# A message-passing layer on a graph: gathered rows transposed 128 edges at a time, and rounds of sums moved behind the next group's products

## The chip, the cores and the metric

The kernel runs on one core of one Trainium2 chip. The time is that of one launch on the device, in microseconds (us), and smaller is better; three runs of the kernel before took 1334.07, 1339.48 and 1347.27 us, with a median of 1339.48 us.

The engines have short names here: PE is TensorE doing matmuls, PEld its loads of weights, DVE is VectorE, ACT ScalarE, POOL GpSimd, SP SyncE. L596 is line 596 of the kernel before. "Issue" as the cause of a wait means that the profile shows nothing that the engine waited for.

## The reference: what is computed

There are 6250 nodes with 128 features (`x`), and 100000 edges with a source and a destination; the edges come sorted by destination. For every edge a small network of three layers turns the two nodes' features into a message; messages are averaged by destination; a second network updates each node; the sum of input and update is normalized. All in float32.

```
msg_in = concat(x[src], x[dst])                      # 100000 x 256
h  = relu(msg_in @ Wm1 + bm1)                        # 100000 x 256
h  = relu(h @ Wm2 + bm2)                             # 100000 x 256
agg = segment_sum(h @ Wm3 + bm3, dst) / max(count, 1)
upd = relu(concat(x, agg) @ Wn1 + bn1) @ Wn2 + bn2
out = layernorm(x + x + upd)
```

## The kernel before, in words

**Preparation.** `msg_in @ Wm1` is the sum of a product that depends on the source alone and one that depends on the destination alone. So the kernel makes two tables in DRAM: `atab` (node times the upper half of Wm1) and `btab` (node times the lower half, split into three bf16 terms). It also transposes the lists of sources so that 128 edges lie on 128 partitions: `src_f` is the list as numbers, copied from the integers at L381 to L383, then transposed by `source_columns` (L455) into `srcT`. The copy at L382 also reorders: within 512 edges, tile `u` gets the 64 edges `u` of the first 256 on partitions 0 to 63, and the 64 edges `u` of the second 256 on partitions 64 to 127.

**The loop over groups.** The edges are cut into 196 groups of 512 (4 tiles of 128; GT = 4). For each group `k` these steps exist:

- `gather` (L530): four indirect DMAs, issued by POOL, bring the group's 4 x 128 rows of `atab` to `rows`, of which there are 4 buffers; they are issued two groups ahead in the program.
- `open_layer` (L558): PE transposes the gathered rows into two PSUM banks. Each bank takes 256 edges. For each half of the hidden units (`c`), for each tile `u`, for each half `h` of the partitions, one transpose of 64 edges x 128 units goes to 64 columns of bank `h`: 2 x 4 x 2 = 16 transposes (L569), each with a load of 128 columns of weights (the data are the weights, the identity is what moves).
- `first_layer` (L574): on top of it four bf16 products (L582) add the destinations' terms; a one-hot matrix `oht` picks the row of `btab` that an edge needs. These contract over 64 partitions. Then ACT takes both banks through four relus to `h1` (L588).
- `second_layer` (L591), for the group before, `k - 1`: 8 float32 matmuls, two to a tile, which the profile shows as 16 records (L596). DVE takes each of the two banks (two tiles) to one of six buffers `h2` with a maximum (L598).
- `some_sums` (L792): a round of sums. PE multiplies a one-hot matrix of 32 nodes with a tile of `h2`, and four windows of 32 nodes lie side by side in one PSUM bank, `sum_bank` (L604, 8 records to a round). After a batch's last round ACT copies the bank to `part` (L609).
- `turn_sums` (L802): three transposes of `part` (L617) on PE; DVE adds the windows to `acc`, the sums of all nodes (L624).
- every fourth group two more tiles of `btab` (L904), up to about the middle of the kernel, and from there on pieces of the node update (`node_stage`, L687; matmuls at L700, L715, L719, L727) in `node_step`.

**What sets the order.** PE's instructions stand in the order of the program, so do those of ACT and DVE in the loop (`manual_schedule`, L411 and L413). For a step `k` below 196 it is: first layer of `k`, the gather of `k + 2`, second layer of `k - 1`, `node_step`, `turn_sums(k)`, `some_sums(k)` (L873 to L889). Which round of which batch falls in which step is set by `deal` (L758): a batch of four groups (groups 0 to 71) has its first round in the step where its last group's second layer stands, one round in the step after, and two in the next; batches of two groups (72 to 147) and of one (148 to 183) come later behind the second layer. There are 196 rounds and 97 turns in all. PE, ACT and DVE meet through semaphores alone.

Of the kernel before, what the change touches and what calls it, by code (L numbers as in the profile page):

```python
# [20 lines left out]
P = 128  # L21
# [15 lines left out]
def kernel(  # L37
# [36 lines left out]
    nc = tc.nc  # L74
# [4 lines left out]
    GT = 4  # L79
    GE = GT * P  # L80
    HE = 2 * P
    NG = -(-E // GE)
# [6 lines left out]
    NQ = 2 * WN  # L89
# [46 lines left out]
    ident = const.tile([P, P], F32, name="ident")  # L136
# [98 lines left out]
    def scratch(at, n, p=P):  # L235
        return acc_flat[:p, at:at + n]
# [52 lines left out]
    halves = [slice(h * NQ, (h + 1) * NQ) for h in range(2)]  # L289
# [9 lines left out]
    with tc.tile_pool(name="prep", bufs=1) as prep, tc.tile_pool(name="pp", bufs=3, space=PSUM) as pp, tc.tile_pool(  # L299
        name="pb", bufs=5, space=PSUM  # L300
    ) as pb:
        src_i, dst_i = (scratch(AT + k * 2 * GE, 2 * GE, R).bitcast(I32) for k in range(2))
        real, src_f, rel = (scratch(AT + k * 2 * GE, 2 * GE, R) for k in (2, 3, 4))
# [45 lines left out]
        def index_work():  # L349
# [29 lines left out]
                              rel.bitcast(BF16)[:, :2 * GE].rearrange("r (s h e) -> r s h e", s=2, h=2))  # L379
            yield  # L380
            for s in range(2):  # L381
                nc.vector.tensor_copy(src_f[:, s * GE:(s + 1) * GE].rearrange("r (u h e) -> r u h e", u=GT, h=2),  # L382
                                      src_i[:, s * GE:(s + 1) * GE].rearrange("r (h u e) -> r u h e", h=2, u=GT))  # L383
            yield
            over = more[:, 1]
            nc.vector.tensor_add(over, most, quad)
# [128 lines left out]
    with edge, tc.tile_pool(name="wk", bufs=2) as wk, tc.tile_pool(  # L515
# [8 lines left out]
        def bank():  # L524
            return banks.tile([P, 2, H], F32, name="bank")

        def flat_bank():
            return bank().rearrange("p t h -> p (t h)")
# [16 lines left out]
        def hot_rows(rb):  # L545
            oht = wk.tile([P, 2, HE], BF16, name="oht")
            nc.vector.tensor_scalar(oht, rb, iota_p, None, op0=ALU.is_equal)
            return oht
# [9 lines left out]
        def open_layer(ag, nt, xt=None):  # L558
            nh = nt // 2
            ph = [bank() for _ in range(nh)]  # L560
            for c in range(HC):
                if xt is not None:
                    for h in range(nh):
                        nc.tensor.matmul(ph[h][:, c, :], w1[:, 0, c * P:(c + 1) * P], xt[:, h * HE:(h + 1) * HE],
                                         start=(c == 0), stop=False, skip_group_check=True)
                    continue
                for u in range(GT):
                    for h in range(nh):
                        nc.tensor.matmul(ph[h][:, c, u * NQ:(u + 1) * NQ], ag[halves[h], u, c * P:(c + 1) * P],  # L569
                                         ident[halves[h], halves[h]], is_transpose=True,  # L570
                                         start=(c == 0 and u == 0), stop=False, skip_group_check=True)
            return ph

        def first_layer(ag, bw, oht, nt, nk, ph=None):  # L574
# [65 lines left out]
        def make_hot(p):  # L640
            ohts[p] = hot_rows(rels[p // 2][:, 2 * (p % 2):2 * (p % 2) + 2])
            make_nodes(p)

        def make_nodes(p):
            ohs[p] = hot_nodes(dloc[:, 2 * p:2 * p + 2, :].rearrange("p g j -> p (g j)"), 2, iota_n)
# [146 lines left out]
        def some_sums(k):  # L792

            for gs, t, n in rounds.pop(k, ()):
                windows = [w for g in gs for w in units_of(g)]
                if t == 0:
                    sum_banks[gs[0]] = flat_bank() if k > NG else p3.tile([P, 2 * H], F32, name="sum_bank")
                sum_tile(sum_banks[gs[0]], windows, t, n)
                if t == n - 1:
                    parts[gs[0]] = part_of(sum_banks.pop(gs[0]), len(windows)), len(windows)  # L800

        def turn_sums(k):  # L802
            for g in turns_at.pop(k, ()):
                part, nw = parts.pop(g)
                pt = turned(part, nw)
                add_up(pt, load_bases(uniti[0:1, unit_at[g]:unit_at[g] + nw], nw, ENG.DVE))
# [50 lines left out]
        for g in range(-4, NG + 14, 2):  # L857
            for i in range(g + 4, min(g + 6, NG)):
                terms[i] = fetch(load_bases(tilei[0:1, i * GT:(i + 1) * GT], NTS[i], ENG.SP), nk_of(i))
            if g < -2:  # L860
                continue
            if (g + 2) % 4 == 0 and g + 6 < NG:
                rels[(g + 6) // 4] = places((g + 6) // 4)
            if g < 0:
                continue
            if g == 0:
                first_step()
            for k in (g, g + 1):
                if k < NG:
                    s = st[k] = {}  # L870
                    if k == 1:
                        xts[1] = open_layer(None, NTS[1], xts[1])
                    s["h1"] = first_layer(rows.pop(k, None), terms.pop(k), ohts[k // 2][:, k % 2], NTS[k], nk_of(k),  # L873
                                          xts.pop(k, None))
                    if k == 0:
                        next_rows()
                    if k == 2:
                        nc.scalar.copy(*pace(5))
                if 2 * XS <= k + 2 < NG:
                    rows[k + 2] = gather(sources(k + 2))  # L880
                if k % 2 == 0 and k + 2 < NG:
                    make_hot(k // 2 + 1)
                if 0 <= k - 1 < NG:
                    second_layer(st.pop(k - 1)["h1"], h2s[(k - 1) % len(h2s)], NTS[k - 1])
                if k < NG:
                    node_step(k)
                if k <= NG:
                    turn_sums(k)
                some_sums(k)  # L889
                if k > NG:  # L890
                    turn_sums(k)
                if k % 2 == 0 and 2 <= k and k + 5 < NG:
                    nc.vector.tensor_copy(*pace(k + 5))
                if k >= NG:
                    node_step(k)
            if g < 6:
                clear(8)
            if g == 0:
                more_rows()
            t0 = B_EARLY + (g - B_FROM) // 2  # L900
            if g >= B_FROM and (g - B_FROM) % 4 == 0 and t0 < NT:
                pbt = bank()
                for a in range(min(2, NT - t0)):
                    nc.tensor.matmul(pbt[:, a, :], xT[:, (t0 + a) * P:(t0 + a + 1) * P], w1[:, 1, :],  # L904
                                     start=True, stop=True)
                b_terms(t0, pbt, b_rows, b_rest)
            if g == 18:
                late_weights()
            if g == 60:
                made_weights()  # L910
            if g == NG + 2:
                with tc.high_priority():
                    again = nc.values_load(
                        again_i[0:1, 0:1], min_val=0, max_val=1,
                        skip_runtime_bounds_check_because="0 or 1, by its computation")
# [8 lines left out]
        with tc.If(again > 0, preferred_fallthrough_block=True, label="again"):  # L924
            with tc.For_i(0, NG, 1) as g:
# [13 lines left out]
                with tc.For_i(0, more, 1):  # L939
# [8 lines left out]
                    ag, bw = gather(idx), fetch(load_bases(ti, GT, ENG.SP), 2)  # L948
# [44 lines left out]
```

## Time and profile before

| | us |
|---|---|
| median of three runs | 1339.48 |
| lowest and highest run | 1334.07, 1347.27 |
| the profiled execution's own time | 1338.36 |
| its span, from the first to the last instruction | 1336.6 |
| PE busy | 1236.1 (10031 matmul records) |
| PE loading weights | 925.5 |
| POOL busy | 748.7 |
| DVE busy | 618.2 |
| ACT busy | 441.9 |
| granted TensorE clock, mean | 0.981 |

How to read the views: a row of the groups gives line, engine, operation, the tiles written and read, shape and count, then busy time in us and the mean of one in ns, then the idle time of the engine ahead of it and what ended most of that. A row of the timeline gives a start and a length in us, with what was merged and how often; lengths on PE reach to the modelled end of the last matmul, so neighbours overlap. A row of the windows gives the busy us of each engine in a stretch and in brackets the number of instructions. Matmuls are pipelined: a mean of 392 ns is the time from entering to leaving, not what one adds to the stream.

### The profile page before, as it was taken

To read this page: it belongs to the slowest core of one execution; us is meant where nothing else is said; L and a number is where in the kernel's file an instruction comes from. 1 tells how busy PE (TensorE), PEld (TensorE's weight loads), DVE (VectorE), ACT (ScalarE), POOL (GpSimd) and SP (SyncE) were. 2 spreads that over 40 slices of the span, in tenths; PEclk is the share of its full clock that TensorE was granted. 3 is DMA by queue.
4 is the path that set the end of the run, shared out by engine and by line. 5 is a ranking of instruction groups with operands and counts; after the bars stand their busy time and mean duration, and the time that the engine had idled before them with its cause. 6 is when DMAs were issued, how large, how long until landed. Compare 5 with 4: busy or idle time off the path is not lost.

```text
span 1336.6 us, 27771 instructions
## 1 busy us (share of the span) xinstructions
PE 1236.1 (92%) x10031; PEld 925.5 (69%) x10032; DVE 618.2 (46%) x1551; ACT 441.9 (33%) x1102; POOL 748.7 (56%) x795
## 2 busy tenths in 40 slices
PE   9779998998999999999899999999999999999997
PEld 7556666666666666676677777777777777777675
DVE  6443333433334333434466554444445556556553
ACT  4432323323323323333333423333233333333331
POOL 2366665665665666656555465565655555555550
PEclk9879999999999999999999999999999999999998
DMA  8544434444434434434444344444444434443330
GB/s 287 177 125 134 132 108 127 130 115 129 133 106 128 135 107 125 134 106 131 126 118 119 114 125 128 118 120 129 118 118 118 115 109 118 109 123 110 106 91 4
DMA packets 107617, 163.90 MB, mean 123 GB/s; under 512 B 26367, under 2 KB 71549, under 8 KB 107457
## 3 DMA queue, kind: packets, MB, share of 16 engines
q0 software_dynamic: 37504, 102.29, 27.7%
q1 hardware_dynamic: 69425, 59.50, 14.0%
q8 instruction: 82, 1.34, 0.4%
q14 instruction: 62, 0.51, 0.1%
q10 hardware_dynamic: 544, 0.26, 0.1%
HBM read 142.48 MB, written 19.86 MB: 121 GB/s over the span
## 4 chain that ended last, share of the span: by engine, by line
PE 89%; issue 7%; DVE 2%; another core or an unknown queue 1%; DMA 1%; ACT 0%; SPq 0%; DVEq 0%
PE bank L596 54%; PE bank L569 9%; PE sum_bank L604 9%; PE bank L582 4%; PE bank L617 2%; PE pbt L431 2%; PE bank L727 2%; PE bank L700 2%; PE bank L719 2%; PE bank L715 2%; PE bank L904 1%; PE pt L448 0%; DVE acc L660 0%; DVE x_sb L598 0%
## 5 line engine op out<-in xcount | busy, mean ns | idle before, releaser
L596 PE MATMUL bank<-w,h 128*128 128x256 f32 x3128 | 768.7, 392 | 67.2 <-issue 64.6
L596 PEld LDWEIGHTS bank<-w,h 128*128 128x128 f32 x3128 | 581.7, 192 | 212.3 <-issue 131.1
L533 POOL DMA_INDIRECT rows<-atab,srcT x392 | 374.9, 956 | 260.6 <-issue 90.4
L533 POOL DMA_INDIRECT rows<-atab,srcP x384 | 364.2, 949 | 277.9 <-issue 126.5
L588 ACT ACTIVATE h<-bank,b 128x256 f32<-128x256 f32 x782 | 306.5, 476 | 395.6 <-remote 189.3
L598 DVE TENSOR_TENSOR x_sb<-bank,nb 128x512 f32<-128x512 f32 x263 | 181.0, 691 | 401.7 <-PE bank L596 233.7
L598 DVE TENSOR_TENSOR h_more<-bank,nb 128x512 f32<-128x512 f32 x128 | 88.3, 692 | 177.5 <-PE bank L596 75.0
L569 PEld LDWEIGHTS bank<-ident,rows 64*128 64x128 f32 x3096 | 112.7, 140 | 77.7 <-issue 56.8
L569 PE MATMUL bank<-ident,rows 64*128 64x64 f32 x3096 | 139.3, 230 | 0.0
L624 DVE TENSOR_TENSOR acc<-acc,bank 128x96 f32 x382 | 96.7, 253 | 51.7 <-PE bank L569 16.5
L604 PE MATMUL sum_bank<-x_sb,oh 128*32 128x257 f32 x1044 | 104.1, 393 | 3.0 <-issue 1.6
L609 ACT COPY part<-sum_bank 128x257 f32<-128x257 f32 x96 | 35.8, 373 | 197.0 <-PE bank L582 75.4
L582 PE MATMUL bank<-oht,terms 64*128 64x128 bf16 (+1 forms) x1132 | 82.6, 237 | 14.5 <-issue 10.9
L604 PE MATMUL sum_bank<-h_more,oh 128*32 128x257 f32 x512 | 59.1, 391 | 1.2 <-DVE h_more L598 0.6
L604 PEld LDWEIGHTS sum_bank<-x_sb,oh 128*32 128x32 f32 x1044 | 28.1, 108 | 41.7 <-issue 34.1
L582 PEld LDWEIGHTS <-terms 64*128 64x128 bf16 x1132 | 44.1, 97 | 16.1 <-issue 13.8
L617 PE MATMUL bank<-ident,part 128*128 128x128 f32 (+1 forms) x291 | 47.3, 271 | 0.5 <-ACT part L609 0.5
L745 ACT ACTIVATE y<-y,sh,rs 128x128 f32<-128x128 f32 (+3 forms) x50 | 22.1, 487 | 67.0 <-DVE sh L743 26.6
L695 DVE RECIPROCAL x_sb<-x_sb 128x256 f32<-128x256 f32 (+3 forms) x26 | 43.0, 1655 | 0.9
L617 PEld LDWEIGHTS bank<-ident,part 128*128 128x128 f32 (+1 forms) x291 | 36.6, 139 | 9.3 <-ACT part L609 1.0
L552 DVE TENSOR_TENSOR oh<-iota_n,dloc 128x256 f32<-128x256 f32 x98 | 40.8, 417 | 3.6 <-ACT dloc L838 3.6
L737 ACT ACTIVATE sd<-mv,eps 128x2 f32<-128x2 f32 (+3 forms) x26 | 7.7, 295 | 97.6 <-DVE mv L735 49.5
(157 smaller groups left out, 625.0 us busy)
## 6 DMA issues: line engine op xcount, KB each, us to landing
terms<-btab SPq DMA_DIRECT2D x566, 32.0 KB
places<-reltab SPq DMA_DIRECT2D x98, 128.0 KB
btab<-x_sb SPq DMA_DIRECT2D x10, 768.0 KB
rows<-atab,srcT POOLq DMA_INDIRECT x392
atab<-acc SPq DMA_DIRECT2D x12, 512.0 KB
rows<-atab,srcP POOLq DMA_INDIRECT x384
xr<-in_x_dram SPq DMA_DIRECT2D x23, 128.0 KB
out_dram<-y SPq DMA_DIRECT2D x23, 128.0 KB
```

Source lines behind the costliest of these rows:

```text
L533: nc.gpsimd.indirect_dma_start(out=ag[:, j, :], out_offset=None, in_=atab[:, :], in_offset=bass.IndirectOffsetOnAxis(ap=idx[:, j:j + 1], a ...
L552: nc.vector.tensor_tensor(oh[:, :ng].rearrange("p g j n -> p (g j) n"), iota.to_broadcast([P, ng * GT, WN]), dl.rearrange("p (j o) -> p j ...
L569: nc.tensor.matmul(ph[h][:, c, u * NQ:(u + 1) * NQ], ag[halves[h], u, c * P:(c + 1) * P], ident[halves[h], halves[h]], is_transpose=True, ...
L582: nc.tensor.matmul(ph[h][:, c, k * n:(k + 1) * n], bw[halves[h], k, c * P:(c + 1) * P], oht[halves[h], k * n:(k + 1) * n], start=False, st ...
L588: nc.scalar.activation(h1[:, c, h * HE:(h + 1) * HE], ph[h][:, c, :], AF.Relu, bias=b1[:, c:c + 1])
L596: nc.tensor.matmul(ph2[:, j - j0, :], h1[:, c, j * P:(j + 1) * P], w2[:, c, :], start=(c == 0), stop=(c == HC - 1))
L598: nc.vector.tensor_tensor(h2[:, j0:j0 + 2, :H], ph2, nb2.to_broadcast([P, 2, H]), op=ALU.max)
L604: nc.tensor.matmul(pg[w * WN:(w + 1) * WN, :H + 1], oh, h2, start=(t == 0), stop=(t == total - 1), skip_group_check=True)
L609: nc.scalar.copy(part[:nw * WN], pg[:nw * WN, :H + 1])
L617: nc.tensor.matmul(pt[:, c, :q], rows, ident[:q, :q], is_transpose=True, start=True, stop=True, skip_group_check=True)
L624: nc.vector.tensor_add(window, window, pt[:, :, j * WN:(j + 1) * WN])
L695: nc.vector.reciprocal(rc, rc)
```

## The change

Three edits. The transposes of gathered rows become 8 of 128 edges x 128 units, each over all 128 partitions, and tile `j` goes to columns of bank `j // 2`. For this the copy of the sources leaves the edges in their order. And in a step `k` below 196 the rounds that stood at the end of step `k - 1` now stand behind the first layer of `k`, ahead of the second layer of `k - 1`; from step 196 on the rounds of the step itself come behind the second layer as well, and the turns come last in every step.

```diff
@@ index_work
             for s in range(2):
-                nc.vector.tensor_copy(src_f[:, s * GE:(s + 1) * GE].rearrange("r (u h e) -> r u h e", u=GT, h=2),
-                                      src_i[:, s * GE:(s + 1) * GE].rearrange("r (h u e) -> r u h e", h=2, u=GT))
+                nc.vector.tensor_copy(src_f[:, s * GE:(s + 1) * GE], src_i[:, s * GE:(s + 1) * GE])
@@ open_layer
-                for u in range(GT):
-                    for h in range(nh):
-                        nc.tensor.matmul(ph[h][:, c, u * NQ:(u + 1) * NQ], ag[halves[h], u, c * P:(c + 1) * P],
-                                         ident[halves[h], halves[h]], is_transpose=True,
-                                         start=(c == 0 and u == 0), stop=False, skip_group_check=True)
+                for j in range(nt):
+                    nc.tensor.matmul(ph[j // 2][:, c, j % 2 * P:(j % 2 + 1) * P], ag[:, j, c * P:(c + 1) * P],
+                                     ident, is_transpose=True, start=(c == 0 and j % 2 == 0), stop=False,
+                                     skip_group_check=True)
@@ the loop over groups
+                some_sums(k - 1)
                 if 0 <= k - 1 < NG:
                     second_layer(st.pop(k - 1)["h1"], h2s[(k - 1) % len(h2s)], NTS[k - 1])
                 if k < NG:
                     node_step(k)
-                if k <= NG:
-                    turn_sums(k)
-                some_sums(k)
-                if k > NG:
-                    turn_sums(k)
+                if k >= NG:
+                    some_sums(k)
+                turn_sums(k)
```

On PE, around the first round of a batch of four groups, the order before is this (L596 is the second layer, L604 the round, L569 the transposes, L582 the destinations' products; `h_2766` is the `h1` of the group before):

```order
L596 MATMUL bank<-w_151,h_2766 128x256 x8
L604 MATMUL sum_bank<-h_more,oh 32x257 x2
L604 MATMUL sum_bank<-x_sb,oh 32x257 x2
L569 MATMUL bank<-ident,rows 128x64 x16
L582 LDWEIGHTS terms
L582 MATMUL bank<-oht,terms 128x256
...
L596 MATMUL bank<-w_151,h_2859 128x256 x8
```

The same place with the change (with two lines fewer ahead, so L594 is the second layer, L602 the round, L567 the transposes, L580 the products):

```order
L594 MATMUL bank<-w_151,h_2516 128x256 x8
L567 MATMUL bank<-ident,rows 128x128 x8
L580 LDWEIGHTS terms
L580 MATMUL bank<-oht,terms 128x256
...
L602 MATMUL sum_bank<-h_more,oh 32x257 x2
L602 MATMUL sum_bank<-x_sb,oh 32x257 x2
L594 MATMUL bank<-w_151,h_2611 128x256 x8
```

The round has moved past the transposes and the products of the next group, 16 transposes have become 8 of twice the width, and the products now stand between transposes and round instead of between transposes and second layer.

On ACT, where a batch ends, the order before is this (L588 are the relus of the first layer, L609 the copy of the finished sums, L256 a copy for `btab`):

```order
L588 ACTIVATE h_2988<-bank,b_153 128x256 x4
L609 COPY part<-sum_bank 128x257
L588 ACTIVATE h_3047<-bank,b_153 128x256 x4
L256 CAST x_sb<-bank 128x2x256
L259 CAST x_sb<-x_sb 128x2x256
```

With the change (L586 are the relus, L607 the copy):

```order
L586 ACTIVATE h_2720<-bank,b_153 128x256 x4
L586 ACTIVATE h_2765<-bank,b_153 128x256 x4
L607 COPY part<-sum_bank 128x257
L256 CAST x_sb<-bank 128x2x256
L259 CAST x_sb<-x_sb 128x2x256
```

The copy has moved behind the next group's four relus. DVE's and POOL's instructions stand in the same order as before; on SP a few loads ahead of the loop's middle and the stores of the output move by some places.

## The prediction

> **What bounds the kernel now.** First the page's head and its chain of waits:
>
> ```profile
> span 1336.6 us, 27771 instructions
> PE 1236.1 (92%) x10031; PEld 925.5 (69%) x10032; DVE 618.2 (46%) x1551; ACT 441.9 (33%) x1102; POOL 748.7 (56%) x795
> PE 89%; issue 7%; DVE 2%; another core or an unknown queue 1%; DMA 1%; ACT 0%; SPq 0%; DVEq 0%
> ```
>
> PE is busy for 92% of the span and carries 89% of the chain that ends last; no other engine comes near. So what the change adds to PE counts, unless PE has idle time that it can go into. The costliest groups, then the timeline of PE through one step that runs without a stall, show what PE does with a group:
>
> ```profile
> L596 PE MATMUL bank<-w,h 128*128 128x256 f32 x3128 | 768.7, 392 | 67.2 <-issue 64.6
> L569 PE MATMUL bank<-ident,rows 64*128 64x64 f32 x3096 | 139.3, 230 | 0.0
> 604.18 3.92 PE L596 MATMUL bank<-w,h 128*128 128x256 f32 x16
> 608.02 0.64 PE L604 MATMUL sum_bank<-x_sb,oh 128*32 128x257 f32 x8
> 608.60 0.71 PE L569 MATMUL bank<-ident,rows 64*128 64x64 f32 x16
> 609.15 0.38 PE L582 MATMUL bank<-oht,terms 64*128 64x256 bf16 x4
> 609.46 3.72 PE L596 MATMUL bank<-w,h 128*128 128x256 f32 x16
> 613.01 0.49 PE L617 MATMUL bank<-ident,part 128*128 128x128 f32 x3
> ```
>
> The starts are what counts: from 604.18 to 609.46 a whole group passes in 5.28 us, and its 16 transposes take 608.60 to 609.15, 0.55 us. 3096 of them at 16 to a group are 193.5 groups (two groups open otherwise, one is half as long).
>
> But the groups pass more slowly than that. Windows of the whole loop, PE and PEld busy and the number of records first, then the same for L596 alone, 16 records to a group:
>
> ```profile
> 250.00:350.00 100.00, 91.78 (x734) 65.31 (x734) 37.03 (x80) 31.23 (x76) 60.56 (x65) 1.00 0.43 125
> 650.00:750.00 100.00, 97.62 (x825) 78.15 (x825) 60.24 (x151) 35.56 (x92) 52.99 (x56) 1.00 0.42 119
> 750.00:850.00 100.00, 95.07 (x844) 73.85 (x843) 50.76 (x131) 34.83 (x92) 58.21 (x62) 1.00 0.42 120
> 150.00:650.00 500.00, 462.88 (x3658) 328.51 (x3658) 189.58 (x424) 157.05 (x385) 304.85 (x322) 0.99 0.42 124
> 650.00:1250.00 600.00, 568.94 (x4944) 444.98 (x4943) 319.66 (x825) 202.61 (x531) 340.36 (x358) 1.00 0.42 118
> 250.00:350.00 100.00, 63.02 (x258) 46.94 (x258) 1.00 0.43 125
> 650.00:750.00 100.00, 52.74 (x224) 41.30 (x224) 1.00 0.42 119
> 750.00:850.00 100.00, 59.11 (x248) 45.68 (x249) 1.00 0.42 120
> 150.00:650.00 500.00, 319.65 (x1277) 236.67 (x1275) 0.99 0.42 124
> 650.00:1250.00 600.00, 342.92 (x1438) 265.84 (x1439) 1.00 0.42 118
> ```
>
> From 150 to 650 us 1277 / 16 = 79.8 groups pass, 6.27 us each, with PE idle for 37.1 us, 0.46 to a group. From 650 to 1250, where the node update has joined, 89.9 groups take 6.67 us each with 31.1 us idle, 0.35 to a group. The idle time is of one sort: stops of up to a microsecond inside L596 that end in "issue" (64.6 of the 67.2 us in its row above), as here:
>
> ```profile
> 615.73 1.33 PE L596 MATMUL bank<-w,h 128*128 128x256 f32 x5 [0.16 <-issue]
> 618.09 0.38 PE L596 MATMUL bank<-w,h 128*128 128x256 f32 x1 [1.02 <-issue]
> 619.58 1.67 PE L596 MATMUL bank<-w,h 128*128 128x256 f32 x7 [1.12 <-issue]
> ```
>
> What makes them no view says. One thing can be read off: they shrink where a group has more work. With 16.1, 15.5 and 14.0 groups in the windows at 250, 750 and 650 us, PE's busy time to a group is 5.69, 6.13 and 6.97 us, and its idle time 0.51, 0.32 and 0.17. From the first to the second 0.19 of 0.44 us is taken up by idle time (43%), from the second to the third 0.15 of 0.84 (18%). I take a third.
>
> **The change part by part.** *The transposes.* 16 of 64 edges become 8 of 128. The trace has the new form, 128 x 128 in float32, eight in a row, and a passage from full-height float32 matmuls to L582:
>
> ```profile
> 38.54 0.81 PE L431 MATMUL pbt<-w,xT 128*128 128x256 f32 x3
> 39.19 1.04 PE L465 MATMUL px<-ident,acc 128*128 128x128 f32 x8
> 46.88 1.99 PE L564 MATMUL bank<-acc,w 128*128 128x256 f32 x8
> 48.81 0.39 PE L582 MATMUL bank<-oht,terms 64*128 64x256 bf16 x4
> L465 PE MATMUL px<-ident,acc x8: 272/272/273, 39.2 to 40.0; 128*128 128x128 f32 x8
> ```
>
> The last of the eight takes 0.27 us to leave, so they enter (1.04 - 0.27) / 7 = 0.11 us apart, and eight cost 0.88 us where sixteen cost 0.55. The sixteen are cheap because the two halves of the partitions run side by side.
>
> *The seams.* Where PE goes over to another part of the array the trace shows a bubble. A matmul of 256 columns enters 0.22 us after the one ahead ((3.72 - 0.38) / 15 at L596) and leaves 0.38 after it entered, so it lets the next in 0.16 before it leaves. The round's last leaves at 608.02 + 0.64 = 608.66 and so lets go at 608.50; the old transposes start at 608.60, a bubble of 0.10. The new ones follow second layer, turn or L904, which use the whole array as they do: L431's last leaves at 39.35, lets go at 39.19, and there L465 starts, with no bubble. In return L582 gets one, which now follows the old transposes at once: L564's last leaves at 48.87, lets go at 48.71, and L582 starts at 48.81, 0.10 later. The round's other seams, to L596 and to L582, change partners but not in number. So to a group: before 0.10 + 0.55 = 0.65, now 0.88 + 0.10 = 0.98, **+0.33 us; over 193.5 groups +63.9 us**. The new form's price is measured on this chip in a stream; its bounds are the rounding of the rows, 0.31 to 0.35 (60 to 68 us).
>
> *The moved rounds.* The first round of a batch of four needs the maximum that DVE has just been handed (L598); before, it stood right behind the second layer that feeds DVE. PE's waits at L604 for it, and the rows of ACT for the other end of the batch:
>
> ```profile
> DVE x_sb L598: 4.9, 5
> DVE h_more L598: 2.2, 4
> L588 ACT ACTIVATE h<-bank,b 128x256 f32<-128x256 f32 x782 | 306.5, 476 | 395.6 <-remote 189.3
> L609 ACT COPY part<-sum_bank 128x257 f32<-128x257 f32 x96 | 35.8, 373 | 197.0 <-PE bank L582 75.4
> ```
>
> These 7.1 us can go at most, since DVE now has transposes and products, over 1 us, to finish in; the least is nothing, if another stop takes their place. I take 4 off. The price of the move: `part` is now copied behind four relus of the next group, 4 x 306.5 / 782 = 1.57 us, and then 0.37. The turn that waits for it comes behind the second layer, 609.46 to 613.01 = 3.55 us of PE, so 1.6 us of cover are left; if they were gone, a tenth of a microsecond would cost 97 turns 10 us. Behind a waiting turn stand the next group's transposes, and POOL waits for their buffers. I take nothing. No DMA, no load of a register and no instruction of DVE or POOL moves past another; SP's few moved stores are waited for by nobody in the loop.
>
> *The copy of the sources* is two casts before the loop, each within one microsecond of DVE beside PE's table products; a plain one may be shorter or not, within 1 us, and lies off the path. Nothing.
>
> *Sum:* 63.9 - 4 = +60 us of work on PE, of which a third, 20, goes into idle time: +40. Against the profiled execution: 1336.6 + 40 = 1376.6 of span, 1.8 around it (1338.36 - 1336.6), and 1.1 from there to the median of the runs shown (1339.48): **1380 us, 3% slower**. With 18 to 43% taken up and the transposes' bounds the forecast's own range is 1372 to 1395.
>
> **The rivals.** *Nothing is taken up.* The stops could come with the clock on the wall, whatever PE has to do; then all 60 to 64 us show: 1400 to 1403. For it: they are found in windows of every kind. Against it: their share falls as the work rises.
>
> *All of it is taken up.* Something that is not PE could pace the loop at 6.27 us (POOL and its gathers, say, with 304.85 us busy for 79.8 groups, 3.8 each, and a pause behind every one). Then +0.33 fits into 0.46 and 0.35 idle: 1340, within 1%. Against it: the second stretch has another pace, and in its fullest window only 0.17 is idle.
>
> *Faster: PE is short of instructions, not of time.* In the first stretch PE gets 7316 records in 500 us, 68 ns to each. A group loses 16 records (8 loads, 8 matmuls) of 92. If the stops come from feeding PE, fewer records fill its queue sooner, and the moved round no longer holds the queue up behind a wait. Then the 68.2 us idle in these 1100 us go, 78 over the loop's 1259 us (from 52.8 to 1312.1 us): 1336.6 + 60 - 78 + 2.9 = 1321. It decides only if more than nine tenths of the stops go. Against it: in the second stretch records come at 61 ns, and the 16 transposes pass at 34 ns each with their loads. The Trainium skill, page "TensorE: Matmul & The Clock Gate", section "Wait — 56ns, not 53.3ns?", says that a sequencer decoding in software spends about 62 ns per matmul, which binds when the array's work is shorter. By that figure, as an estimate, 46 matmuls of a group would need 2.8 us, well under 6.27, so that the loop as a whole would not be bound by it; the transposes' own 34 ns disagree with it too.
>
> *Loads that no longer overlap.* Eight full-height loads could each wait for the transpose ahead: 139 ns as in the row below, on top of 0.11, makes 2.0 us instead of 0.88, and +215 us more, 1595.
>
> ```profile
> L617 PEld LDWEIGHTS bank<-ident,part 128*128 128x128 f32 (+1 forms) x291 | 36.6, 139 | 9.3 <-ACT part L609 1.0
> ```
>
> The Trainium skill, the same page, section "The mechanism" in Part 3, has a rule that says so: loads overlap running matmuls only where the row groups differ. The row of L465 speaks against it: with a load to each, they enter 0.11 us apart.
>
> **How the numbers follow.** The forecast 0.46; nothing taken up 0.24; all of it 0.14; faster 0.13; loads in series 0.03. Within 1% is about what a measurement of this kernel can tell from no change, since the three runs spread over 1%. Faster by over 1% 0.13, the same 0.14, slower 0.46 + 0.24 + 0.03 = 0.73. The range for 8 in 10 goes from the faster case's price, 1320, leaving out half of it, to 1410, above the case without take-up: 1320 to 1410.
>
> **What would show it.** Right: the new transposes number 1548, eight in a row about 1.04 us long in the timeline; the products (L582) begin 0.98 us after the first of them; a step without stall takes 5.6 us; PE's busy time up by some 60 us, its idle time down by some 20, most of it in L596's "issue"; the waits of L604 for DVE near zero; L617 without waits for `part`. Wrong: a pitch of the transposes far from 0.11; idle time in "issue" that is unchanged (1403) or gone (1321); groups at 6.27 us as before in the first stretch (1340); new waits of PE for ACT at L617.

## The result, and the profile after

The changed kernel takes 1454.28 us (four runs, 1451.15 to 1461.07) against 1339.28 us for the kernel before: ratio 1.0866, interval 1.0829 to 1.0902. It is slower, as forecast, but by 115 us instead of 40, and beyond the range (1320 to 1410). The ratios in this document are of the runs that the record counts as fast, the medians of all runs. The head of its page, the chain of waits and two of its groups:

```profile
span 1454.3 us, 24724 instructions
PE 1317.2 (91%) x8483; PEld 1017.8 (70%) x8484; DVE 608.1 (42%) x1551; ACT 437.2 (30%) x1102; POOL 750.4 (52%) x795
PE 82%; issue 6%; another core or an unknown queue 5%; ACT 3%; DVE 3%; DMA 1%; SPq 0%; DVEq 0%; ACTq 0%
L594 PE MATMUL bank<-w,h 128*128 128x256 f32 x3128 | 750.1, 393 | 8.5 <-issue 8.4
L567 PE MATMUL bank<-ident,rows 128*128 128x128 f32 x1548 | 215.0, 281 | 13.2 <-issue 12.9
```

PE's busy time is up by 81 us (1236.1 to 1317.2), and the rest of the span, in which PE is idle, has grown too, from 100 to 137 us, where the forecast had it shrink by 20. The stops inside the second layer are all but gone (64.6 us in "issue" before, 8.4 now), but others have come. What PE waited for, in us, with the number of times and the longest:

```profile
PE bank L615 <- ACT part L607: 42.5, 15, 4.4
PE bank L580 <- issue: 18.3, 23, 1.3
PE sum_bank L602 <- issue: 16.7, 20, 2.4
PE bank L567 <- issue: 12.9, 24, 1.7
PE bank L615 <- issue: 10.2, 7, 3.4
```

The turn (L615) waits 42.5 us for `part`, where it waited 0.5 us before. Where no stop falls into a step, the change is what the prediction worked out. The timeline of PE, in the same kernel:

```profile
610.88 3.72 PE L594 MATMUL bank<-w,h 128*128 128x256 f32 x16
614.44 1.04 PE L567 MATMUL bank<-ident,rows 128*128 128x128 f32 x8
615.41 0.39 PE L580 MATMUL bank<-oht,terms 64*128 64x256 bf16 x4
615.73 0.64 PE L602 MATMUL sum_bank<-x_sb,oh 128*32 128x257 f32 x8
616.30 3.72 PE L594 MATMUL bank<-w,h 128*128 128x256 f32 x16
```

The eight transposes come right behind the second layer, last 1.04 us, and the products start 0.97 after the first of them. Now the pace over the loop, all engines first (PE and PEld busy ahead), then L594 alone with 16 records to a group:

```profile
150.00:650.00 500.00, 462.04 (x2902) 351.02 (x2901) 176.04 (x401) 149.04 (x369) 291.17 (x305) 0.97 0.40 117
650.00:1250.00 600.00, 553.46 (x3756) 434.23 (x3755) 274.93 (x710) 177.66 (x473) 307.72 (x323) 0.97 0.38 107
150.00:650.00 500.00, 288.30 (x1225) 0.97 0.40 117
650.00:1250.00 600.00, 313.31 (x1300) 0.97 0.38 107
```

A group takes 500 / (1225 / 16) = 6.53 us in the first stretch (6.27 before) and 600 / (1300 / 16) = 7.38 in the second (6.67 before). Most of the loss lies where the node update has joined, the stretch with the least idle time before.

### The profile page after: what moved, and what is told of

Same layout as the page of the kernel before. It is cut to its first block, busy times and chain, and to the rows that moved or that the text cites. A ratio compares the mean times of both kernels' runs of the same rounds, so it can differ in the third digit from the quotient of the medians.

```text
span 1454.3 us, 24724 instructions
## 1 busy us (share of the span) xinstructions
PE 1317.2 (91%) x8483; PEld 1017.8 (70%) x8484; DVE 608.1 (42%) x1551; ACT 437.2 (30%) x1102; POOL 750.4 (52%) x795
## 4 chain that ended last, share of the span: by engine, by line
PE 82%; issue 6%; another core or an unknown queue 5%; ACT 3%; DVE 3%; DMA 1%; SPq 0%; DVEq 0%; ACTq 0%
PE bank L594 44%; PE bank L567 12%; PE sum_bank L602 8%; PE bank L580 5%; PE bank L615 3%; ACT h L586 3%; PE pbt L430 2%; PE bank L725 2%; PE bank L717 2%; PE bank L698 1%; PE bank L901 1%; PE bank L713 1%; DVE x_sb L596 1%; DVE acc L622 1%
## 5 line engine op out<-in xcount | busy, mean ns | idle before, releaser
L594 PE MATMUL bank<-w,h 128*128 128x256 f32 x3128 | 750.1, 393 | 8.5 <-issue 8.4
L594 PEld LDWEIGHTS bank<-w,h 128*128 128x128 f32 x3128 | 591.0, 194 | 171.2 <-issue 83.5
L586 ACT ACTIVATE h<-bank,b 128x256 f32<-128x256 f32 x782 | 307.2, 475 | 539.5 <-remote 169.3
L596 DVE TENSOR_TENSOR x_sb<-bank,nb 128x512 f32<-128x512 f32 x263 | 177.8, 690 | 509.8 <-PE bank L594 152.2
L567 PE MATMUL bank<-ident,rows 128*128 128x128 f32 x1548 | 215.0, 281 | 13.2 <-issue 12.9
L567 PEld LDWEIGHTS bank<-ident,rows 128*128 128x128 f32 x1548 | 187.5, 146 | 30.8 <-issue 18.5
L596 DVE TENSOR_TENSOR h_more<-bank,nb 128x512 f32<-128x512 f32 x128 | 86.2, 689 | 242.7 <-remote 107.3
L602 PE MATMUL sum_bank<-x_sb,oh 128*32 128x257 f32 x1044 | 112.0, 409 | 18.0 <-issue 13.8
L580 PE MATMUL bank<-oht,terms 64*128 64x128 bf16 (+1 forms) x1132 | 85.5, 247 | 20.5 <-issue 18.3
L615 PE MATMUL bank<-ident,part 128*128 128x128 f32 (+1 forms) x291 | 51.9, 290 | 55.9 <-ACT part L607 42.5
L615 PEld LDWEIGHTS bank<-ident,part 128*128 128x128 f32 (+1 forms) x291 | 35.5, 145 | 74.4 <-ACT part L607 49.5
L580 PEld LDWEIGHTS <-terms 64*128 64x128 bf16 x1132 | 35.3, 96 | 58.3 <-issue 54.6
L602 PEld LDWEIGHTS sum_bank<-x_sb,oh 128*32 128x32 f32 x1044 | 29.2, 110 | 48.8 <-issue 33.1
L602 PE MATMUL sum_bank<-h_more,oh 128*32 128x257 f32 x512 | 59.9, 392 | 3.3 <-issue 2.8
L607 ACT COPY part<-sum_bank 128x257 f32<-128x257 f32 x96 | 37.4, 389 | 75.5 <-remote 45.8
L720 ACT ACTIVATE x_sb<-bank,bu 128x256 f32<-128x256 f32 (+3 forms) x52 | 21.0, 456 | 79.5 <-remote 44.9
```

Of the source, the lines that this page charges most:

```text
L567: nc.tensor.matmul(ph[j // 2][:, c, j % 2 * P:(j % 2 + 1) * P], ag[:, j, c * P:(c + 1) * P], ident, is_transpose=True, start=(c == 0 and j ...
L580: nc.tensor.matmul(ph[h][:, c, k * n:(k + 1) * n], bw[halves[h], k, c * P:(c + 1) * P], oht[halves[h], k * n:(k + 1) * n], start=False, st ...
L586: nc.scalar.activation(h1[:, c, h * HE:(h + 1) * HE], ph[h][:, c, :], AF.Relu, bias=b1[:, c:c + 1])
L594: nc.tensor.matmul(ph2[:, j - j0, :], h1[:, c, j * P:(j + 1) * P], w2[:, c, :], start=(c == 0), stop=(c == HC - 1))
L596: nc.vector.tensor_tensor(h2[:, j0:j0 + 2, :H], ph2, nb2.to_broadcast([P, 2, H]), op=ALU.max)
L602: nc.tensor.matmul(pg[w * WN:(w + 1) * WN, :H + 1], oh, h2, start=(t == 0), stop=(t == total - 1), skip_group_check=True)
```

## The experiments

The kernel before does not take the same time everywhere, and that became the main finding. On some chips, here **sort A**, it takes 1337 to 1339 us: the prediction's profile and the result are of this sort, and the runs on chips 10 and 3. On others, **sort B**, it takes 1190 us: chips 2, 6, 11 and 12. PE is busy there for 99% of the span (in the moved rounds alone, which take as long). No numbered chip was used in more than one set of runs, so the record can't tell a lasting difference between chips from a state that a chip is in for some minutes; "sort" stands for either. Each kernel is compared with the kernel before that ran beside it:

| | sort A (before 1338) | sort B (before 1190) |
|---|---|---|
| wide transposes alone | 1350.17, +13 | 1278.56, +89 |
| moved rounds alone | 1406.29, +69 | 1189.81, 0 |
| both: the change | 1455.05, +118 | 1253.35, +63 |
| the change, turns a step later | 1454.95, +118 | 1263.56, +74 |
| before, no gathers | 1202.62, -136 | - |
| moved rounds, no gathers | - | 1189.40, -1 |
| the change, no gathers | - | 1253.50, +64 |

**The parts alone, on sort B.** The first edit is the transposes and the copy of the sources without the move; the second is the move without the transposes:

```diff
+                some_sums(k - 1)
                 if 0 <= k - 1 < NG:
                     second_layer(st.pop(k - 1)["h1"], h2s[(k - 1) % len(h2s)], NTS[k - 1])
...
-                if k <= NG:
-                    turn_sums(k)
-                some_sums(k)
-                if k > NG:
-                    turn_sums(k)
+                if k >= NG:
+                    some_sums(k)
+                turn_sums(k)
```

> The kernel before with the wide transposes alone; rounds and turns stand as before. Theory A (the turn that now follows its round after one second layer only is what costs beyond the transposes' own time, since PE's signals of finished work reach ACT up to 7 us late): the price of the transposes, 0.31 us a group, shows, so 1385 to 1400 us; PE waits less than 3 us for part at the turn; idle time in issue stays near 80 us. Theory B (the wide transposes themselves make the stops worse, whatever the order): 1430 or more, with the stops spread over all lines.

> The kernel before with the moved rounds alone; sixteen half transposes to a group. Theory A: PE waits some 40 us for part at the turn, and then runs at a lower clock for a while, so 1385 to 1405 us. Theory B: the moved rounds are harmless or save a few us, 1330 to 1345, and the waits for part stay below 10 us.

Measured: 1278.56 us (ratio 1.0744, 1.0726 to 1.0762) and 1189.81 us (1.0003, 0.9993 to 1.0012), beside 1189.65. The forecasts were made for sort A and can't be judged by these runs. On this chip the moved rounds cost nothing, and the transposes cost more without them than with them. PE's timeline of the wide transposes alone shows why:

```profile
610.16 0.64 PE L602 MATMUL sum_bank<-h_more,oh 128*32 128x257 f32 x8
610.73 1.09 PE L567 MATMUL bank<-ident,rows 128*128 128x128 f32 x8
611.75 0.40 PE L580 MATMUL bank<-oht,terms 64*128 64x128 bf16 x8
```

Here the transposes stand behind a round: it lets its follower in at 610.16 + 0.64 - 0.16 = 610.64, so they start 0.09 late, and the products follow after 1.02 instead of 0.97. The round has its own seam to the second layer ahead of it as before. Together that is an estimated 0.14 us at each of the 166 places where a round stands ahead, 23 us, of the 25 between 1278.56 and 1253.35 (the changed kernel on sort B, below).

**The turn a step later.** Of the changed kernel, on both sorts:

```diff
+                if k <= NG:
+                    turn_sums(k - 1)
                 some_sums(k - 1)
...
                 if k >= NG:
                     some_sums(k)
-                turn_sums(k)
+                    turn_sums(k)
```

> The changed kernel with each turn moved behind the next group's first layer, ahead of the rounds there, so that a whole step lies between the last round of a batch and its turn, as before the change. Theory A: the waits for part (42.5 us) go to below 3 us and what follows from them too: 1390 to 1410 us. Theory B: the stop only moves to the next instruction that waits, 1440 to 1455.

On sort B it takes 1263.56, ten more than the change (an estimate: 97 turns, most of which now stand between products and round, with one seam of 0.10 us more each). The sort A run follows below.

**No gathers.** Only the first four gathers of the loop are made, and all later groups use their rows again; 190 of 194 gathers are left out.

```diff
-                    rows[k + 2] = gather(sources(k + 2))
+                    if k + 2 < 6:
+                        saved[k + 2] = gather(sources(k + 2))
+                    rows[k + 2] = saved[2 + k % 4]
```

> The changed kernel with only the first four gathers of the loop; all later groups use their rows again, so 190 of 194 gathers with their DMA are left out. Theory A, with the further claim that it is the gathers that hold PE's signals back: ACT and DVE start within 0.1 us of the end of the matmuls they wait for, PE's idle time in issue and for part together falls from 126 to below 30 us, and the time to 1290 to 1330. If the gathers have no part in it (the delay is PE's own, or comes with its stream of instructions): idle time stays above 80 us and the time above 1400.

> The changed kernel with only the first four gathers, once more. Where the kernel before takes 1338: theory E: 1255 to 1270, which is the kernel before without gathers (1203) and the transposes' own 55 to 65 us; otherwise above 1300.

Both ran on sort B: 1253.57 and 1253.50, the same as the change with its gathers (1253.35). Next came the changed kernel once more, and the same edit in the kernel before, both on sort A:

> The changed kernel as it is. The last four runs found the kernel before at 1190 us with PE busy for 99% of its span, where the profile of the prediction has 1339 us and 92%. Theory C: the change has two prices, the transposes' own, which shows everywhere, and the stops, which show only where signals of PE come late. If the kernel before takes 1190 here too: 1255 to 1270 (the changed kernel with late turns took 1264, and the turn costs nothing without late signals), PE 99% busy, no wait for part above 1 us. If it takes about 1340: 1454 as before, with PE at 91%. Theory B (the moved turn itself costs 40 us and more): 1300 or more wherever the kernel before takes 1190.

> The kernel before with only the first four gathers of the loop; 190 of 194 gathers are left out. If the kernel before takes 1190 beside it: 1180 to 1190, since nothing waits for a gather there. If it takes about 1340: with the gathers as what holds PE's signals back, idle time of PE falls from 100 to below 30 us and the time to 1180 to 1230; if the delay is PE's own, above 1310.

The changed kernel took 1455.79 us (1437.02 to 1465.12; ratio 1.0780, 1.0695 to 1.0866). The kernel before without gathers took 1202.62 against 1338.19 (0.8974, 0.8935 to 0.9013), as forecast. Without gathers 136 us are gone and PE's waits with them; its head and its longest wait now:

```profile
PE 1179.5 (98%) x10031; PEld 917.5 (76%) x10032; DVE 612.0 (51%) x1551; ACT 440.9 (37%) x1102; POOL 25.2 (2%) x35
PE bank L596 <- issue: 4.8, 6, 1.1
```

The move of the rounds in a kernel without gathers:

> The kernel before with the moved rounds, and only the first four gathers (190 left out). Theory E: the moved rounds cost only by what the gathers hold back, so as the kernel before without gathers, 1195 to 1210. If the moved rounds have a price of their own on this chip: 1250 or more.

It ran on sort B: 1189.40 against 1189.98, no difference. On sort A it was not run.

**The parts alone on sort A,** with the change beside them on the same chip:

> The wide transposes alone, once more, since the chip decides: where the kernel before takes 1190 they cost 89 us (0.41 us a group by the seams of this order, 80 us, and some more). If the kernel before takes 1338 here: theory D (the transposes cost PE time only, and the stops come from late signals at the moved turn): 1385 to 1420, PE waits for part below 3 us. Theory B (the transposes make the stops worse): 1430 or more.

> The moved rounds alone, once more: nothing where the kernel before takes 1190. If the kernel before takes 1338 here: theory D: the turn stands one second layer behind its round, signals come up to 7 us late, so PE waits some 40 us for part and runs slower behind long waits: 1380 to 1400. Theory B: no difference by more than 1%, 1325 to 1350.

> The changed kernel with the turns one step later, once more. If the kernel before takes 1338 here: theory D: the 43 us of waits for part and what follows from them go, 1390 to 1415, against 1455 for the changed kernel beside it. Theory B: 1440 to 1460, with the stops at other lines. Where the kernel before takes 1190: 1264 as before.

> The changed kernel beside the three others, on their chip. If the kernel before takes 1338: 1455 again. If it takes 1190: theory D says 1250 to 1256, the transposes' own 0.31 to 0.33 us a group and nothing for the moved turn; theory B 1280 or more, above the 1279 of the wide transposes alone.

Beside 1337.38: 1350.17 (ratio 1.0105, 1.0040 to 1.0171), 1406.29 (1.0464, 1.0387 to 1.0541), 1454.95 (1.0874, 1.0805 to 1.0943), 1455.05 (1.0870, 1.0817 to 1.0923). No theory had the first: the wide transposes alone, 89 us of work on sort B, cost 13 here (four runs from 1339.41 to 1359.59). The second lies 6 us above theory D's range, but for another reason than the one it gave: PE waits 9.2 us for `part`, not 40. The page of the wide transposes alone, its engines, its second layer and its windows:

```profile
PE 1279.4 (96%) x8483; PEld 985.1 (74%) x8484; DVE 616.1 (46%) x1551; ACT 438.6 (33%) x1102; POOL 748.7 (56%) x795
L594 PE MATMUL bank<-w,h 128*128 128x256 f32 x3128 | 732.0, 387 | 7.1 <-issue 6.8
150.00:650.00 500.00, 300.55 (x1293) 0.99 0.43 123
650.00:1250.00 600.00, 335.68 (x1440) 1.00 0.42 119
```

80.8 and 90.0 groups pass, where the kernel before passed 79.8 and 89.9: the loop keeps its pace. This execution's span is 1.0 us longer than that of the prediction's profile (1337.6 and 1336.6): PE's busy time is up by 43 us and its idle time down by 42, and the second layer, whose pauses are in part counted as busy, takes 732.0 us instead of 768.7. So most of PE's added work has gone into its stops. The moved rounds alone cost 69 us, and 105 on top of the wide transposes. With the turn a step later the wait for `part` is gone (0.6 us are left), but not a microsecond of the time: the stops have gone elsewhere, as theory B had it for this run. PE's longest waits of that kernel (sort A):

```profile
PE bank L567 <- issue: 34.8, 48, 1.8
PE bank L580 <- issue: 23.4, 31, 1.9
PE sum_bank L602 <- issue: 17.2, 23, 1.8
PE sum_bank L602 <- DVE x_sb L596: 8.3, 4, 5.2
```

So theory D, that the turn's cover is the price of the move, has fallen.

**Plain loads for gathers, and ACT's order.** The first puts one load by SP in place of a group's four gathers, always rows that stand one behind the other in the table, so that the sources are left out. The second keeps the rounds where the change has them on PE, but issues the copy to `part` ahead of the four relus, from a line in `first_layer` between the products and the relus:

```diff
-                    rows[k + 2] = gather(sources(k + 2))
+                    rows[k + 2] = ld.tile([P, GT, H], F32, name="rows")
+                    at = (k * 32) % 5600
+                    nc.sync.dma_start(rows[k + 2], atab[at:at + GE, :].rearrange("(j p) h -> p j h", p=P))
```

```diff
+            if between is not None:
+                some_sums(between)
```

> The kernel before with a plain load by SP in place of each group's four gathers: the same bytes to the same tiles in pieces of the same 1 KB, but always rows that lie in a row, so the sources are left out; POOL issues nothing in the loop. If the kernel before takes 1338 beside it. Theory E (POOL's indirect gathers hold PE's signals and its instructions back): 1200 to 1230, as without gathers. Theory F (any DMA of that size does): 1310 to 1345.

> The moved rounds alone, but the copy to part is issued ahead of the next group's four relus, as before the change; on PE everything stands as in the moved kernel. If the kernel before takes 1338 beside it. Theory G (ACT's order costs: the copy now stands behind relus that wait for a late signal): 1335 to 1355. Theory H (it is the place of the rounds among PE's instructions): 1390 to 1410 as with the moved rounds alone (1406).

> Plain loads in place of the gathers in the kernel before (the sources are left out), once more: 1199 where the kernel before takes 1190. If it takes 1338 beside it: theory E (POOL's indirect gathers hold PE back): 1200 to 1230; theory F (any DMA of that size does): 1310 to 1345.

> The moved rounds with the copy to part ahead of the relus, once more: no difference where the kernel before takes 1190. If it takes 1338 beside it: theory G (ACT's order costs): 1335 to 1355; theory H (the place among PE's instructions): 1390 to 1410.

> The moved rounds with the copy to part ahead of the next group's relus, a third time, for a chip where the kernel before takes 1338: theory G (ACT's order costs): 1335 to 1355; theory H (the place among PE's instructions): 1390 to 1410, as the moved rounds alone (1406). Where the kernel before takes 1190: 1190.

All five ran on sort B and decide nothing for sort A: 1199.38 and 1200.35 for the plain loads, 1190.59, 1190.43 and 1190.55 for the copy ahead of the relus, beside 1189.94 to 1190.08. The change beside two of these:

> The changed kernel. If the kernel before takes 1190 beside it: 1250 to 1264, the transposes' own 0.32 us a group, 62 us, and up to 10 us for gathers (1264 with late turns, 1253.5 without gathers). If it takes 1338: 1455 again.

1253.35 against 1189.94 (1.0538, 1.0521 to 1.0556): on sort B the change costs 63.4 us.

## Why the prediction was wrong, point by point

**The transposes' price was right.** The sum gave 63.9 us from 0.11 us a transpose and one seam that is only exchanged. On sort B, where PE has no idle time to hide anything, the change costs 63.4, and the timeline has the 1.04 and 0.97 us. The step without a stall is 5.42 us, not 5.6: the 5.28 that the prediction took for a clean step of the kernel before held a stop, since its second layer to round took 3.84, where 3.56 to the next full-array line and a seam of 0.10 make 3.66.

**"A third is taken up" failed.** On sort A, where the profile came from, the wide transposes alone show 13 of their 89 us, about a seventh, where the forecast let two thirds show. So PE's work did not set the pace of the loop. The rival "all of it is taken up", which gave 1340, comes nearest, and the cycle that it names, POOL and its gathers, fits: the prediction's argument against it, that the second stretch has another pace, doesn't hold, since both stretches kept their paces (6.19 and 6.67 us). POOL's timeline in the kernel before:

```profile
290.60 0.95 POOL L533 DMA_INDIRECT rows<-atab,srcP  x1 [1.45 <-PE bank L596]
291.85 0.94 POOL L533 DMA_INDIRECT rows<-atab,srcP  x1 [0.30 <-issue]
293.10 0.95 POOL L533 DMA_INDIRECT rows<-atab,srcP  x1 [0.30 <-issue]
294.35 0.95 POOL L533 DMA_INDIRECT rows<-atab,srcP  x1 [0.30 <-issue]
296.92 0.94 POOL L533 DMA_INDIRECT rows<-atab,srcT  x1 [1.62 <-PE bank L596]
```

Four gathers start 1.25 us apart, and the next four begin 2.57 after the last start, released by PE: 3.75 + 2.57 = 6.32 us, the pace of a group (6.27). In the trace 140 of the loop's 193 intervals between two such fours are 2.25 to 2.75 us. The gathers by themselves do not make this pace. On sort B four of them take as long (3.76 us from the first to the last start, in the median of the moved rounds alone), but the next four begin 1.34 us after the last start, in the median, instead of 2.48. What sort A adds is the pause, which ends with a signal from PE.

**"These 7.1 us can go at most, ... I take 4 off" is the step that failed, with the price of the move, "I take nothing".** On sort A the moved rounds cost 69 us alone and 105 on top of the transposes. The prediction looked at one engine's cover for one copy and priced it at zero, because 1.6 us were left over by the durations. The cover was not 1.6 us, because on sort A ACT and DVE learn late that PE is done; but the cover of this one copy is not the whole price, since the time stays the same with the turn a step later. The gain of 4 was misread too. Its rows add the waits of PE's weight loads to those of its matmuls; the matmuls alone waited 1.8 us for DVE in the kernel before:

```profile
PE sum_bank L604 <- DVE x_sb L598: 1.2, 1, 1.2
PE sum_bank L604 <- DVE h_more L598: 0.6, 2, 0.4
```

With the change this wait grew instead of going, to 3.7 + 0.5 us for the matmuls and from 7.1 to 11.3 us with the loads. Around one of the waits for `part`, first PE, then POOL, ACT and DVE of the changed kernel:

```profile
262.54 3.72 PE L594 MATMUL bank<-w,h 128*128 128x256 f32 x16
269.76 0.55 PE L615 MATMUL bank<-ident,part 128*128 128x128 f32 x3 [3.50 <-ACT part L607]
270.14 1.03 PE L901 MATMUL bank<-w,xT 128*128 128x256 f32 x4
271.01 1.81 PE L567 MATMUL bank<-ident,rows 128*128 128x128 f32 x8
```

```profile
262.87 0.95 POOL L532 DMA_INDIRECT rows<-atab,srcP  x1 [0.30 <-PE sum_bank L602]
264.12 0.94 POOL L532 DMA_INDIRECT rows<-atab,srcP  x1 [0.30 <-issue]
265.37 0.94 POOL L532 DMA_INDIRECT rows<-atab,srcP  x1 [0.30 <-issue]
266.62 0.95 POOL L532 DMA_INDIRECT rows<-atab,srcP  x1 [0.30 <-issue]
273.09 0.95 POOL L532 DMA_INDIRECT rows<-atab,srcT  x1 [5.52 <-PE bank L567]
```

```profile
262.92 1.57 ACT L586 ACTIVATE h<-bank,b 128x256 f32<-128x256 f32 x4 [3.71 <-PE sum_bank L602]
269.33 0.38 ACT L607 COPY part<-sum_bank 128x257 f32<-128x257 f32 x1 [4.84 <-remote]
```

```profile
269.43 1.29 DVE L596 TENSOR_TENSOR x_sb<-bank,nb 128x512 f32<-128x512 f32 x2 [8.13 <-remote]
```

The round ahead of this second layer was done by 262.61 and ACT's relus by 264.49, yet the copy to `part` starts at 269.33. The first eight matmuls of the second layer are done by 262.54 + 7 x 0.22 + 0.38 = 264.46 (264.54 in their own records), yet DVE's maximum, which needs only them, starts at 269.43, with DVE idle for 8 us ahead of it. It is the signal that is late, not DVE: the trace also records when PE's counter is raised, on which both engines wait, and the raises for the round and for the two halves of the second layer, done by 262.61, 264.54 and 266.26, stand together at 269.31, 269.40 and 269.50. All of this lies under four gathers, and ends 2.7 us after the last one's start. PE, which has done all it could, stands for 3.5 us, and then runs at half its pace for a while: the eight transposes of 271.01 last 1.81 us, against 1.04. The same place of the changed kernel on sort B, PE, POOL and DVE:

```profile
265.13 3.72 PE L594 MATMUL bank<-w,h 128*128 128x256 f32 x16
```

```profile
265.15 0.95 POOL L532 DMA_INDIRECT rows<-atab,srcT  x1 [1.94 <-PE bank L567]
266.40 1.14 POOL L532 DMA_INDIRECT rows<-atab,srcT  x1 [0.30 <-issue]
267.85 0.95 POOL L532 DMA_INDIRECT rows<-atab,srcT  x1 [0.30 <-issue]
```

```profile
268.89 0.69 DVE L596 TENSOR_TENSOR x_sb<-bank,nb 128x512 f32<-128x512 f32 x1 [0.97 <-PE bank L594]
```

Gathers run here too, and DVE starts 0.04 us after PE's last matmul (265.13 + 3.72 = 268.85). Over the whole trace, a maximum of DVE counts as late where it starts more than 0.5 us after the eighth matmul that it needs and after DVE's own instruction before it:

| of 389 maxima | late | sum of their delays, us |
|---|---|---|
| sort A: before | 87 | 141 |
| wide transposes alone | 65 | 121 |
| moved rounds alone | 149 | 290 |
| the change (the result's profile) | 132 | 414 |
| the change, turns later | 113 | 308 |
| before, no gathers | 1 | 2 |
| sort B: wide alone, moved alone, the change | 0 | 0 |

The records of PE's counter bear this out: a raise stands within 0.2 us ahead of 87 of the 87 late starts before the change, 147 of 149 with the moved rounds and 131 of 132 with the change, and over 0.4 us behind the end of the matmul. So late signals are there on sort A with gathers, and, but for one, neither on sort B nor without gathers. Of the 87 before the change, 67 come 2 to 3 us after the start of the last gather issued; of those with the moved rounds 38, and with the change 65, and most of the others come within 1.5 us of a gather's start. With the moved rounds there are more late signals, and they are longer. That the 69 and 105 us are made of them is not shown by itself: the two go together, and where the signals are prompt, the move costs nothing (1189.81, 1189.40). Nor is it shown how PE's own stops in "issue" hang together with late signals; without gathers both are gone. Why the move makes more of them late is open. It isn't the turn's place (1454.95 with the turn later). Whether it is the rounds' place among PE's instructions or the copy's among ACT's is not known: the run that would tell ran three times, each time on sort B, where the move costs nothing. Nor have plain loads on sort A, so it is open whether POOL's indirect gathers or any transfer of that size would hold the signals back.

**The sum as measured.** The profiled spans differ by 117.7 us. PE's busy time takes 81. If 64 of them are the transposes', as on sort B, 17 are left, of which an estimated 11 are half-pace entries in second layers and transposes (21 us of them against 10 before, from the starts in the trace). The remaining 37 are PE idle. The forecast had +64, -4 and -20.

**The rivals.** "Nothing is taken up" ended at 1403, and the range ended just above it, at 1410, since no rival let the idle time grow. That is why the range was too narrow: the unknown stops, whose cause "no view says", were given a price below zero and up to nothing, never above. "Faster" took the stops to come from the feeding of PE with many records. The wide transposes alone have the fewer records, and the stops at the second layer did fall from 64.6 to 6.8 us, yet the time did not; and without gathers these stops are gone with all the old records (4.8 us), so the number of records is not what makes them. The rival of the loads that no longer overlap is ruled out by the 1.04 us of the eight transposes.

**What the prediction would have seen.** The late signals stood in its own trace: DVE's and ACT's starts against the ends of the matmuls they wait for. It read PE's stops on PE alone, found "issue", and went on with durations.

## What to carry to other kernels

Where stops end in "issue", put the starts of the waiting engines beside the ends of what they wait for, before any cover is reckoned in durations: a cover of 1.6 us is none where a signal may be 5 us late, as in the place shown. A bound that is busy for 92% need not set the pace; look for the engine whose cycle fits the loop's, here POOL's four gathers and the pause behind them, and ask what keeps that cycle in step before work is moved past it. An unknown stop has a price on both sides of zero.

## What the runs showed of the hardware that was not expected

The same kernel takes 12% longer on one sort than on the other: medians of 1337 to 1339 us on three occasions, and of 1189.65 to 1190.08 on four chips. The difference goes away but for about 13 us when the gathers are left out (1202.62 for the kernel before on sort A, 1189.40 for the kernel with moved rounds on sort B). So on sort A gathers cost 136 us by what they do to others, though their packets take as long in sum on both. The rows of the gathers' queue, the kernel before on sort A and the moved rounds alone on sort B (packets, MB, share of 16 engines' span):

```profile
q0 software_dynamic: 37504, 102.29, 27.7%
```

```profile
q0 software_dynamic: 37504, 102.29, 31.0%
```

27.7% of 1336.6 us are 370, and 31.0% of 1187.4 are 368. What holds the signals back was not found.

Behind one wait of 3.5 us, or several of about a microsecond, the traces of sort A show PE entering matmuls at half the pace (0.43 us from one matmul of the second layer to the next instead of 0.22, and eight transposes in 1.81 us instead of 1.04), in stretches whose granted clock is 0.5. The mean granted clock falls with it: 0.981 in the kernel before and 0.959 in the changed kernel, which has 0.997 on sort B.
